# A graph layer on one core: the last but one node group's feed-forward moved behind the last edge pair, and another edge pair gathered ahead

## The chip, the cores and the metric

One core of a Trainium2 chip runs the program. Its engines work side by side, each through its own queue in order: PE (TensorE, matrix products and transposes), DVE (VectorE), ACT (ScalarE), POOL (GpSimd, here the issuer of gathers, DMAs whose rows are picked by a list of indices) and SP (SyncE, the issuer of all other DMAs). The metric is the device time of one execution in microseconds; several executions are timed and their median is taken. Separately one execution is profiled.

## What is computed

A graph attention layer over N = 12500 nodes and E = 400000 edges, sorted by destination, 128 features in 8 heads of 16, 32 features per edge. Cut to what matters:

```
h   = relu(layernorm(x))
x_l = ln1(h) @ W_l            x_r = ln1(h) @ W_r
per edge:  m     = leaky_relu(x_l[src] + x_r[dst] + edge_attr @ W_e)
           alpha = sum over a head of (m * att)
per node:  out   = sum(exp(alpha - max) * x_l[src]) / sum(exp(alpha - max))
           (each node has also an edge to itself, with the mean edge_attr)
h   = h + out + bias
y   = x + h + gelu(ln2(h) @ W1 + b1) @ W2 + b2
```

## The kernel before

Nodes are kept in 98 tiles of 128, edges are worked on in **pairs**: pair c holds edges 512 c to 512 c + 511, in four columns of 128. There are 782 pairs, 0 to 781, and the last has one column only.

**Prologue.** `tile_gnn` normalises x, multiplies it by W_l and writes the rows x_l to DRAM (`xl_dram`). While that runs, 29 pairs are served another way, since their rows of x_l do not exist yet: POOL gathers rows of x itself (`raw_gather`, L288) and they are stored in `raw_dram`. `raw_pairs` (L131) says which pairs: 24 at steps of 32 pairs (40, 72, ..., 744, 776) and `RAW_MORE` = 5 more, each 8 after one of the first of these (48, 80, 112, 144, 176).

**The edge loop.** `window_edges` writes its order out by hand. Time is counted in rounds r; the table `stages` says which step works in round r on which pair, so that on every engine the steps of several pairs alternate:

- r = c - 4, `gather` (L926): POOL issues four gathers from `xl_dram`, one per column, into the row buffer `xs` (12 buffers). For one of the 29 pairs SP loads the finished rows from `late_dram` instead (L921).
- r = c, `combine` (L980, L984): PE transposes the gathered rows and adds the products of the edge features and of the window of x_r.
- r = c + 1, `slope` (ACT, L998) and `bend` (DVE, L1003), the leaky relu; r = c + 2, `apart` (L991) and `score` (L1008) on PE; r = c + 3, `lowest` (DVE, L1014; L1017 for the short last pair) and `weigh` (ACT, the exponential, L1025); r = c + 4, `turn` (PE transposes, L1033); r = c + 5, `keep_turned` (ACT, L1038); r = c + 6, `collect` (PE, the weighted sums, L1047); r = c + 7, `own_heads` (DVE, L1056 and L1062) and `put` (SP, L1073), which writes each unit's sums into one of two `state` arrays in DRAM; writes into one array follow each other.

The last pair is combined in round 781, collected in 787, and put in 788.

**Rows gathered ahead.** For each of the 29 pairs, `raw_steps` (L609 to L691) runs twelve steps in twelve rounds, starting 17 rounds before the pair's own: load from `raw_dram` (SP), statistics, root, scale, relu, four transposes on PE (L651), copy and squares, variance, root, four products on PE (L672), rows, store to `late_dram` (SP).

**Node groups.** When all edges of a group of nodes have been put, the group's state is read back and the rest of the layer is done for it. `node_groups` makes 25 groups: three tiles, then 23 of four, then the end group of three. Ordinary groups follow the table `steps`, one step a round: `f_load` (x_l, x_r and x, on SP), `f_order` (ACT copy), `f_z` (PE, L1152 and L1156), `f_bend`, `f_state` (SP, L1123), `f_score`, `f_low` (L1187 to L1193), `f_exp`, `f_den`, `f_out` (DVE, L1214 to L1224), `f_h`, `f_stats`, `f_root`, `f_scale` (ACT, `hn`, L1260), `f_turn` (PE, L1271), `f_turned` (ACT, L1286), two `f_up` (PE, L1297), two `f_gelu` (ACT, L1312), `f_down` (PE, L1322), `f_store` (DVE, L1335 to L1339), `f_put` (SP, L1342). Their offsets run from -4 to 17, with `f_out` at 5 and `f_scale` at 9; the group of round 740 is the last of them.

The last but one group has round 772 and follows a denser table, `soon`: `f_load` at 768, `f_state` at 772, `f_low` and `f_exp` at 773, `f_den` and `f_out` at 774, `f_h` and `f_stats` at 775, `f_root` and `f_scale` at 776, `f_turn` at 777, the ups and gelus at 778 and 779, `f_down` at 780, `f_store` and `f_put` at 781. The end group has round 790 and follows `last_steps`: `f_load` at 772 up to `f_kept` at 777 (f_biases, L1136 and L1138, at 775), then `f_state` at 790 and all the rest at 791.

**PSUM rings and buffers.** `z`, `ab`, `pt_ps` and `acc` are rings of two banks each. Node steps borrow from them: `bank_of` takes one of `acc` if nothing else is said, and `f_out` one of `ab`. Most tiles of a node group have one buffer and are shared by all groups; the end group has its own `xo`, `x` and `sc`.

Of the kernel before, what the change touches and what calls it, by code (L numbers as in the profile page):

```python
# [53 lines left out]
AHEAD = 4  # L54
WAHEAD = 3
XR_STEPS = 6
RAW_MORE = 5
RAW_SHIFT = 8
RAW_STEPS = 12
TURN_AT = 13  # L60
# [48 lines left out]
def node_groups(nt):  # L109

    last = GN - 1
    first = (nt - last) % GN
    at = ([0] if first else []) + list(range(first, nt, GN))
    return [(t, n - t) for t, n in zip(at, at[1:] + [nt])]


def edges_per_node(nt, n_edges):
    return -(-n_edges // (nt * P))
# [7 lines left out]
def xr_round(t0, nt, n_edges):  # L126

    first = (t0 * P - CW) * edges_per_node(nt, n_edges) // U - SPARE
    return first // UP - WAHEAD - XR_STEPS - 1


def raw_pairs(nt, n_edges):

    n_pr = -(-n_edges // (UP * U))
    at = [xr_round(t, nt, n_edges) + XR_STEPS + 1 for t in range(GN, nt, GN)]
    at = at + [r + RAW_SHIFT for r in at[:RAW_MORE]]
    return [(r + RAW_STEPS + AHEAD + 1, r) for r in at if r + RAW_STEPS + AHEAD + 2 < n_pr]


# [9 lines left out]
def tile_gnn(  # L149
# [45 lines left out]
    dc_dram = dram.tile([RP * RU // UP * PW], BF16, name="dc_dram")  # L195
    du_dram = dram.tile([RP * RU * U], BF16, name="du_dram")
    raw = [{"c": c, "i": i, "round": r, "n": UP * KU} for i, (c, r) in enumerate(raw_pairs(NT, n_edges))]
    raw_dram = dram.tile([len(raw), P, UP * KU, P], F32, name="raw_dram")
    late_dram = dram.tile([len(raw), P, UP * KU, XW], F32, name="late_dram")
# [72 lines left out]
    def load_raw():  # L272
        step = GN * P * edges_per_node(NT, n_edges) // (UP * U)
        for part in (raw[: len(raw) - RAW_MORE], raw[len(raw) - RAW_MORE :]):
            assert all(d["c"] == part[0]["c"] + i * step for i, d in enumerate(part))
# [576 lines left out]
def window_edges(  # L852
# [30 lines left out]
    with ExitStack() as es:  # L883
# [218 lines left out]
        groups = [{"t0": t, "n": n, "ts": slice(t, t + n)} for t, n in node_groups(NT)]  # L1102
        end = groups[-1]

        def own_tile(d, name, shape, dt, tag=None, bufs=1):

            if d is end and name in ("xo", "x", "sc"):
                return fin.tile(shape(d["n"]), dt, name=f"end_{name}")
            return fin.tile(shape(GN), dt, name=f"f_{name}", tag=tag or f"f_{name}", bufs=bufs)

        def tiles(name, d, tag=None):
            d[name] = own_tile(d, name, lambda n: [P, n, P], F32, tag)
            return d[name][:, 0 : d["n"]]

        def bank_of(d, name, ring="acc"):
            d[name] = ps2.tile([P, EPR], F32, name=ring)
            return d[name]

        def f_state(d):
            n, ts = d["n"], d["ts"]  # L1120
            d["st"] = own_tile(d, "st", lambda n: [P, 2, n, SW], F32, "big", 3)
            for i in range(2):
                nc.sync.dma_start(d["st"][:, i, 0:n], state[i].rearrange("(t p h) f -> p t (h f)", p=P, h=H)[:, ts, :])  # L1123
# [104 lines left out]
        def f_h(d):  # L1228
            hb = h_sb[:, d["ts"], :].rearrange("p t f -> p (t f)")
            nc.vector.tensor_add(d["sum"], d["sum"], d["o2"])  # L1230
            if d is not end:
                up = d["sum"].rearrange("p (t f) -> p t f", f=P)
                nc.vector.tensor_add(up, up, bias_r[:, None, :].to_broadcast([P, d["n"], P]))
            nc.vector.tensor_add(hb, hb, d["sum"])
# [31 lines left out]
                )  # L1266

        def f_turn(d):
            tp = bank_of(d, "tp")
            for i in range(d["n"]):  # L1270
                nc.tensor.transpose(tp[:, i * P : (i + 1) * P], d["hn"][:, i, :], ident)  # L1271

# [20 lines left out]

        def f_up(k):
            def up(d):
                n, u = d["n"], bank_of(d, f"u{k}")
                nc.tensor.matmul(  # L1297
                    u[:, 0 : n * P],
                    w1_sb[:, k * P : (k + 1) * P],
                    d["hT"][:, 0:n].rearrange("p t f -> p (t f)"),  # L1300
                    start=True,
                    stop=True,
                )

            return up

        def f_gelu(k):
            def gelu(d):
                n = d["n"]
                if k == 0:  # L1310
                    d["gel"] = own_tile(d, "gel", lambda n: [P, 2, n * P], F32, "big", 3)
                nc.scalar.activation(  # L1312
                    d["gel"][:, k, 0 : n * P], d[f"u{k}"][:, 0 : n * P], AF.Gelu, bias=cols[:, 5 + k : 6 + k]
                )

            return gelu

        def f_down(d):
            y = bank_of(d, "y")
            for i in range(d["n"]):  # L1320
                for k in range(2):
                    nc.tensor.matmul(  # L1322
                        y[:, i * P : (i + 1) * P],
                        d["gel"][:, k, i * P : (i + 1) * P],
                        w2_sb[:, k, :],
                        start=(k == 0),
                        stop=(k == 1),
                    )

        def f_store(d):  # L1330
            n = d["n"]
            up = d["y"][:, 0 : n * P].rearrange("p (t f) -> p t f", f=P)
            d["out"] = y = tiles("yo", d, "f_b")
            if d is end:
                nc.vector.tensor_add(y, up, d["x"][:, 0:n])  # L1335
                return
            nc.vector.tensor_add(up, up, d["x"][:, 0:n])
            nc.vector.tensor_add(up, up, h_sb[:, d["ts"], :])
            nc.vector.tensor_add(y, up, b2_r[:, None, :].to_broadcast([P, n, P]))  # L1339

        def f_put(d):
# [41 lines left out]
            (8, f_root),  # L1383
            (9, f_scale),
            (10, f_turn),
            (11, f_turned),
            (12, f_up(0)),
            (13, f_up(1)),
            (13, f_gelu(0)),
            (15, f_down),  # L1390
            (16, f_store),
            (17, f_put),
        )
        up0, up1, gelu0, gelu1 = f_up(0), f_up(1), f_gelu(0), f_gelu(1)
        soon = (
            (-4, f_load),
            (-3, f_order),
            (-2, f_z),
            (-1, f_bend),
            (0, f_state),  # L1400
            (0, f_score),
            (1, f_low),
            (1, f_exp),
            (2, f_den),
            (2, f_out),
            (3, f_h),
            (3, f_stats),
            (4, f_root),
            (4, f_scale),
            (5, f_turn),  # L1410
            (5, f_turned),
            (6, up0),
            (6, gelu0),
            (7, up1),
            (7, gelu1),
            (8, f_down),
            (9, f_store),
            (9, f_put),
        )
        last_steps = (  # L1420
            (-18, f_load),
            (-17, f_order),
            (-16, f_z),
            (-15, f_bend),
            (-15, f_biases),
            (-14, f_score),
            (-13, f_kept),
            (0, f_state),
            (1, f_low),
            (1, f_exp),  # L1430
# [13 lines left out]
            (1, gelu1),  # L1444
            (1, f_down),
            (1, f_store),
            (1, f_put),
        )
# [8 lines left out]
        def in_round(r, table, groups=groups):  # L1457
            for k, f in table:
                for d in groups:
                    if d["round"] + k == r:  # L1460
                        f(d)
# [10 lines left out]
        with tc.manual_schedule():  # L1472
            for r in range(-AHEAD, max(last_round, groups[-1]["round"] + 18)):
                in_round(r, early, groups[:-2])
                for late, f in stages:
                    c = r - late
                    if 0 <= c < n_pr:
                        f(c)
                for late, f in sum_stages:
                    i, off = divmod(r - late, SUM_STEP)  # L1480
                    if off == 0 and 0 <= i < NL:
                        f(i)
                if r > 0 and r % CLEAR == 0 and r // CLEAR < NT // GT:
                    clear(r // CLEAR)
                in_round(r, steps, groups[:-2])
                in_round(r, soon, groups[-2:-1])
                in_round(r, last_steps, groups[-1:])
                in_round(r, enumerate(xr_steps), qs[1:])
                in_round(r, enumerate(raw_steps), raw)
                for late, f in late_stages:  # L1490
                    c = r - late
                    if 0 <= c < n_pr:
                        f(c)
# [354 lines left out]
```

## Time and profile before

| | |
|---|---|
| timed, median of 3 runs | 3979.37 us (3976.93 to 3980.35) |
| the profiled execution, its time | 3979.82 us |
| the profiled execution, its span | 3978.0 us |
| PE busy | 3535.5 us (89%) |
| DVE busy | 2996.7 us (75%) |
| POOL busy | 2961.1 us (74%) |
| ACT busy | 2177.6 us (55%) |
| granted TensorE clock, mean | 0.955 |

The span runs from the first instruction to the last, and the execution's time is 1.8 us longer. Busy shares are means over prologue, edge loop and end. Rows of the timeline give the start in us from the span's beginning, the busy time of a merged run of instructions, engine, line, operation, tiles and count, and in brackets the idle time ahead of it with what ended it. Rows of groups give the total busy time, the mean in ns of one, and the idle time ahead of them with its releasers. Rows of stages give from : to, the length, then each engine's busy time with its number of instructions (for a single line: of that line's engine alone), then the granted clock, the DMA share and GB/s.

### The profile page before, as it was taken

Reading aid. Unit: us, or ns where it says so; the run is one execution under the profiler, and the core shown is the slowest. Engines: PE = TensorE matmul, PEld = TensorE weight load, DVE = VectorE, ACT = ScalarE, POOL = GpSimd, SP = SyncE. Lnnn points to the kernel's source line nnn. Section 1 sums busy time; section 2 is a strip of 40 time slices with the busy share of each in tenths; the row PEclk is TensorE's granted clock in tenths of the full one; section 3 lists DMA queues with packets and bytes.
Section 4 is the critical chain, followed back from the end, with each engine's and each line's share of the span. In section 5 each row is a group of like instructions: output and inputs, shape, how many; then the busy total and the mean of one; then the engine's idle time right before and its main releaser. Section 6 shows DMA issues by size and latency. Waiting matters only on the chain.

```text
span 3978.0 us, 63158 instructions
## 1 busy us (share of the span) xinstructions
PE 3535.5 (89%) x18434; PEld 2235.4 (56%) x18435; DVE 2996.7 (75%) x6282; ACT 2177.6 (55%) x4746; POOL 2961.1 (74%) x3147
## 2 busy tenths in 40 slices
PE   2588899999999999999999999989999999999987
PEld 2355555555555556555665556656565655555554
DVE  6578888888878777777777777777777767767766
ACT  7445545555555545555555555556455555555554
POOL 7777777777777777777777777777777777777772
PEclk9799999999999999999999999999999999999998
DMA  7677777766655555555555555555555555555552
GB/s 207 210 176 175 182 190 179 165 161 154 151 103 114 109 112 112 109 110 108 104 110 115 109 110 111 113 109 108 112 104 107 110 115 97 110 110 100 107 104 63
DMA packets 625309, 502.69 MB, mean 126 GB/s; under 512 B 320174, under 2 KB 522013, under 8 KB 624717
## 3 DMA queue, kind: packets, MB, share of 16 engines
q1 hardware_dynamic: 524381, 281.11, 29.6%
q0 software_dynamic: 100000, 217.32, 27.7%
q8 instruction: 152, 2.49, 0.3%
q14 instruction: 200, 1.64, 0.1%
q10 hardware_dynamic: 576, 0.13, 0.0%
HBM read 432.27 MB, written 65.83 MB: 125 GB/s over the span
## 4 chain that ended last, share of the span: by engine, by line
PE 41%; POOL 20%; DMA 17%; issue 13%; DVE 7%; ACT 1%; SPq 1%; POOLq 0%; DVEq 0%; ACTq 0%
POOL xs L926 17%; DMA xs<-xl_dram,src_sb 14%; PE acc L1047 10%; PE z L984 10%; PE ab L1008 8%; PE pt_ps L1033 7%; PE z L980 4%; POOL raw L288 2%; DVE rec L1014 1%; DMA state<-rec 1%; DVE ea L967 1%; DVE m L1003 1%; PE acc L1322 1%; PE acc L1297 1%; DVE own L1056 1%
## 5 line engine op out<-in xcount | busy, mean ns | idle before, releaser
L926 POOL DMA_INDIRECT xs<-xl_dram,src_sb x3009 | 2842.4, 945 | 917.3 <-issue 790.1
L1025 ACT ACTIVATE p<-ab,rec 128x256 f32<-128x256 f32 x1563 | 654.8, 470 | 1026.9 <-DVE rec L1014 1011.6
L1047 PE MATMUL acc<-xs,pt 128*128 128x136 f32 x6250 | 904.6, 291 | 0.6 <-DVE f_m L1166 0.5
L984 PE MATMUL z<-ea,zw 64*128 64x512 f32 x1564 | 900.4, 656 | 3.8 <-DMA zw<-xr_dram 3.5
L980 PE MATMUL z<-ident,xs 128*128 128x128 f32 x3125 | 575.9, 285 | 291.0 <-DMA xs<-xl_dram,src_sb 260.3
L1056 DVE TENSOR_TENSOR own<-acc,diag 128x272 f32<-128x272 f32 x782 | 342.9, 438 | 652.5 <-PE acc L1047 646.5
L1008 PE MATMUL ab<-m,negrep 128*128 128x512 f32 x1564 | 833.5, 616 | 0.0
L1047 PEld LDWEIGHTS acc<-xs,pt 128*128 128x128 f32 x6250 | 828.8, 201 | 1.1 <-DVE f_m L1166 0.8
L980 PEld LDWEIGHTS z<-ident,xs 128*128 128x128 f32 x3125 | 406.9, 144 | 718.2 <-DMA xs<-xl_dram,src_sb 370.8
L1038 ACT COPY pt<-pt_ps 128x512 f32<-128x512 f32 x782 | 454.8, 582 | 573.1 <-PE pt_ps L1033 562.1
L1033 PEld LDWEIGHTS pt_ps<-ident,p 128*128 128x128 f32 x3125 | 340.5, 145 | 617.9 <-issue 510.1
L1003 DVE TENSOR_TENSOR m<-z,zs 128x512 f32<-128x512 f32 x782 | 532.8, 681 | 103.6 <-ACT zs L998 99.1
L967 DVE TENSOR_SCALAR ea<-dl,nid 32x516 f32<-32x516 bf16 x782 | 582.1, 744 | 29.0 <-DMA dl<-dc_dram 3.7
L1014 DVE TENSOR_REDUCE rec<-ab 128x2 f32<-128x512 f32 x781 | 538.8, 690 | 34.8 <-PE ab L1008 33.4
L1033 PE MATMUL pt_ps<-ident,p 128*128 128x128 f32 x3125 | 534.4, 296 | 2.6 <-ACT pt L1038 1.9
L998 ACT ACTIVATE zs<-z 128x512 f32<-128x512 f32 x782 | 472.0, 604 | 45.4 <-PE z L984 45.4
L1062 DVE TENSOR_REDUCE rec<-own 128x34 f32<-128x272 f32 x782 | 340.8, 436 | 26.7
L991 PE MATMUL ab<-ne,farw 64*128 64x512 bf16 x782 | 307.3, 393 | 31.2 <-ACT p L1025 27.4
L984 PEld LDWEIGHTS z<-ea,zw 64*128 64x128 f32 x1564 | 234.7, 188 | 122.3 <-issue 59.8
L1008 PEld LDWEIGHTS ab<-m,negrep 128*128 128x128 f32 x1564 | 252.8, 200 | 2.3 <-issue 2.3
L973 DVE TENSOR_SCALAR ne<-dl,nid 96x512 bf16<-96x512 bf16 x391 | 145.7, 373 | 12.7 <-DMA dl<-du_dram 0.3
L288 POOL DMA_INDIRECT raw<-in_x,src_raw x116 | 115.3, 994 | 38.8 <-issue 34.4
(206 smaller groups left out, 2163.2 us busy)
## 6 DMA issues: line engine op xcount, KB each, us to landing
ea<-in_ea_t SPq DMA_DIRECT2D x392, 128.0 KB
ea_s<-in_ea_t SPq DMA_DIRECT2D x98, 512.0 KB
xs<-xl_dram,src_sb POOLq DMA_INDIRECT x3009
dl<-dc_dram SPq DMA_DIRECT2D x392, 66.0 KB
state<-rec SPq DMA_DIRECT2D x1563, 9.0 KB
state<-empty SPq DMA_DIRECT2D x28, 504.0 KB
f_st<-state SPq DMA_DIRECT2D x46, 288.0 KB
dl<-du_dram SPq DMA_DIRECT2D x392, 32.0 KB
```

Source lines behind the costliest of these rows:

```text
L926: nc.gpsimd.indirect_dma_start(out=xs[:, j, :], out_offset=None, in_=xl_dram, in_offset=bass.IndirectOffsetOnAxis(ap=src_sb[:, c * KP + j ...
L967: nc.vector.tensor_scalar(d["ea"][rs].rearrange("p (a b) -> p a b", b=OW), d["dl"][rs].rearrange("p (a b) -> p a b", b=OS)[:, :, 0:OW], ni ...
L980: nc.tensor.matmul(z[:, j * P : (j + 1) * P], d["xs"][:, j, 0:P], ident, start=(j == 0), stop=False, is_transpose=True)
L984: nc.tensor.matmul(z[:, :e], d["zw"][rs], d["ea"][rs, :e], start=False, stop=True)
L998: nc.scalar.activation(d["zs"][:, :e], d["z"][:, :e], AF.Copy, scale=SLOPE)
L1003: nc.vector.tensor_tensor(d["m"][:, :e], d["z"][:, :e], d["zs"][:, :e], op=OP.max)
L1008: nc.tensor.matmul(d["ab"][:, :e], negrep.rearrange("p n h -> p (n h)"), d["m"][:, :e], start=False, stop=True)
L1014: nc.vector.tensor_reduce(d["rec"][:, :, CX], d["ab"].rearrange("p (u e) -> p u e", e=U), AX.X, OP.min)
L1025: nc.scalar.activation(d["p"][:, us], d["ab"][:, us], AF.Exp, bias=d["rec"][:, i, CX:SH], scale=-1.0)
L1033: nc.tensor.transpose(d["pt_ps"][:, js], d["p"][:, js], ident)
L1038: nc.scalar.copy(d["pt"][:, :e], d["pt_ps"][:, :e])
L1047: nc.tensor.matmul(d["acc"][:, i, :], d["pt"][:, j * P : (j + 1) * P], d["xs"][:, j, :], start=(j == js[0]), stop=(j == js[-1]),)
```

## The change

1. The list of pairs gathered ahead: pair 776 is dropped and 208 is added (`RAW_MORE` 6, and the last of the steps of 32 cut off). There are still 29.
2. The last but one group's table `soon` is stretched: `f_load` to `f_kept` in rounds 758 to 763, `f_state` at 772, then `f_low`, `f_exp`, `f_den`, `f_out`, `f_h`, `f_stats`, `f_root` one per round from 773 to 779, `f_scale` at 780.
3. Its feed-forward has a table of its own, `after`, counted from the end group's round 790: `f_ready` (an activation on one column that loads the gelu's table), `f_turn` and `f_turned` in 788, ups and gelus in 789, `f_down` and `f_store` in 790, `f_put` in 791. In each round they come ahead of the end group's steps of that round and behind the stages of the pairs.
4. As in the end group, the biases go into h and x early (`f_biases`), x + h is formed in `f_rest`, and `f_store` is then a single add.
5. Its banks come from other rings: `f_turn` and the ups from `z`, `f_down` from `ab`.
6. The end group's early steps move to rounds 764 to 769.

```diff
-RAW_MORE = 5
+RAW_MORE = 6
...
-    at = at + [r + RAW_SHIFT for r in at[:RAW_MORE]]
+    at = at[:-1] + [r + RAW_SHIFT for r in at[:RAW_MORE]]
...
+        def near_end(d):
+            return any(d is g for g in groups[-2:])
...
         def f_h(d):
-            if d is not end:
+            if not near_end(d):
...
-            tp = bank_of(d, "tp")
+            tp = bank_of(d, "tp", "z" if d is groups[-2] else "acc")
...
-                n, u = d["n"], bank_of(d, f"u{k}")
+                n, u = d["n"], bank_of(d, f"u{k}", "z" if d is groups[-2] else "acc")
...
-            y = bank_of(d, "y")
+            y = bank_of(d, "y", "ab" if d is groups[-2] else "acc")
...
         def f_store(d):
-            if d is end:
+            if near_end(d):
                 nc.vector.tensor_add(y, up, d["x"][:, 0:n])
                 return
...
         soon = (
-            (-4, f_load), (-3, f_order), (-2, f_z), (-1, f_bend),
-            (0, f_state), (0, f_score), (1, f_low), (1, f_exp),
-            (2, f_den), (2, f_out), (3, f_h), (3, f_stats),
-            (4, f_root), (4, f_scale), (5, f_turn), (5, f_turned),
-            (6, up0), (6, gelu0), (7, up1), (7, gelu1),
-            (8, f_down), (9, f_store), (9, f_put),
+            (-14, f_load), (-13, f_order), (-12, f_z), (-11, f_bend),
+            (-11, f_biases), (-10, f_score), (-9, f_kept),
+            (0, f_state), (1, f_low), (2, f_exp), (3, f_den),
+            (4, f_out), (5, f_h), (6, f_stats), (7, f_root),
+            (8, f_scale), (8, f_rest),
+        )
+        after = (
+            (-2, f_ready), (-2, f_turn), (-2, f_turned),
+            (-1, up0), (-1, up1), (-1, gelu0), (-1, gelu1),
+            (0, f_down), (0, f_store), (1, f_put),
         )
         last_steps = (
-            (-18, f_load), (-17, f_order), (-16, f_z), (-15, f_bend),
-            (-15, f_biases), (-14, f_score), (-13, f_kept),
+            (-26, f_load), (-25, f_order), (-24, f_z), (-23, f_bend),
+            (-23, f_biases), (-22, f_score), (-21, f_kept),
...
                 in_round(r, soon, groups[-2:-1])
+                for k, f in after:
+                    if end["round"] + k == r:
+                        f(groups[-2])
                 in_round(r, last_steps, groups[-1:])
```

(The tables of the diff are set several entries to a line here.)

More of the change, by code (lines that the diff above doesn't have):

```diff
@@ L1395, in window_edges @@
         soon = (
[L1396 to L1399, printed above, removed]
+            (-14, f_load),
+            (-13, f_order),
+            (-12, f_z),
+            (-11, f_bend),
+            (-11, f_biases),
+            (-10, f_score),
+            (-9, f_kept),
             (0, f_state),
-            (0, f_score),
             (1, f_low),
[L1403 to L1418, printed above, removed]
+            (2, f_exp),
+            (3, f_den),
+            (4, f_out),
+            (5, f_h),
+            (6, f_stats),
+            (7, f_root),
+            (8, f_scale),
+            (8, f_rest),
+        )
+        after = (
+            (-2, f_ready),
+            (-2, f_turn),
+            (-2, f_turned),
+            (-1, up0),
+            (-1, up1),
+            (-1, gelu0),
+            (-1, gelu1),
+            (0, f_down),
+            (0, f_store),
+            (1, f_put),
         )
         last_steps = (
[L1421 to L1427, printed above, removed]
+            (-26, f_load),
+            (-25, f_order),
+            (-24, f_z),
+            (-23, f_bend),
+            (-23, f_biases),
+            (-22, f_score),
+            (-21, f_kept),
             (0, f_state),
```

## The prediction

> **What bounds the kernel now.** I read the costliest groups first, for POOL.
>
> ```profile
> span 3978.0 us, 63158 instructions
> ...
> L926 POOL DMA_INDIRECT xs<-xl_dram,src_sb x3009 | 2842.4, 945 | 917.3 <-issue 790.1
> ```
>
> POOL issues 3009 gathers of rows. The idle time ahead of them is 917.3 / 3009 = 0.305 us each, almost all "issue". So a gather costs 0.945 + 0.305 = 1.25 us and a pair, four of them, 5.0 us. Next, the stages, for these gathers alone, then the POOL timeline.
>
> ```profile
> 200.00:700.00 500.00, 378.04 (x401) 0.95 0.74 180
> ...
> 2200.00:3200.00 1000.00, 756.11 (x801) 0.97 0.54 110
> ...
> 3700.00:3900.00 200.00, 151.21 (x161) 0.97 0.55 113
> ```
> ```profile
> 158.44 0.94 POOL L926 DMA_INDIRECT xs<-xl_dram,src_sb  x1 [0.30 <-issue]
> ...
> 2605.93 0.94 POOL L926 DMA_INDIRECT xs<-xl_dram,src_sb  x1 [0.31 <-issue]
> ...
> 3755.35 0.94 POOL L926 DMA_INDIRECT xs<-xl_dram,src_sb  x1 [0.30 <-issue]
> ...
> 3765.33 0.94 POOL L926 DMA_INDIRECT xs<-xl_dram,src_sb  x1 [0.30 <-issue]
> ...
> 3850.24 0.94 POOL L926 DMA_INDIRECT xs<-xl_dram,src_sb  x1 [0.30 <-issue]
> ...
> 3915.62 0.94 POOL L926 DMA_INDIRECT xs<-xl_dram,src_sb  x1 [0.30 <-issue]
> 3916.87 0.94 POOL L926 DMA_INDIRECT xs<-xl_dram,src_sb  x1 [0.30 <-issue]
> ```
>
> The rate never changes (401 in 500 us, 161 in 200 us) and (3916.87 - 158.44) / 3008 is again 1.25 us: **POOL never stops between its first gather and its last.** The rows above are, in order, the first gather, the last gathers of pairs 509, 747, 749, 766 and 780, and the single gather of 781 (counted back from the end: four a pair, one for 781, none for a pair gathered first). Beside them, TensorE's transposes (L980) of the same pairs:
>
> ```profile
> 2609.54 0.33 PE L980 MATMUL z<-ident,xs 128*128 128x128 f32 x1 [0.89 <-DMA xs<-xl_dram,src_sb]
> ...
> 3762.38 0.81 PE L980 MATMUL z<-ident,xs 128*128 128x128 f32 x4
> ...
> 3766.45 0.60 PE L980 MATMUL z<-ident,xs 128*128 128x128 f32 x4
> ...
> 3770.31 0.60 PE L980 MATMUL z<-ident,xs 128*128 128x128 f32 x4
> ...
> 3852.77 0.33 PE L980 MATMUL z<-ident,xs 128*128 128x128 f32 x1 [0.24 <-DMA xs<-xl_dram,src_sb]
> ...
> 3931.74 0.60 PE L980 MATMUL z<-ident,xs 128*128 128x128 f32 x4
> ...
> 3937.39 0.27 PE L980 MATMUL z<-ident,xs 128*128 128x128 f32 x1
> ```
>
> I call **lag** the time from the start of a pair's last gather to the end of its transposes. It is 3.9 us at pair 509, 7.8 at 747, 5.6 at 749, 2.9 at 766 (TensorE waits for the rows there), but 3932.34 - 3915.62 = 16.7 at 780 and 3937.66 - 3916.87 = 20.8 at 781. Up to 766 the kernel goes at POOL's pace; over the last fifteen rounds TensorE falls 18 us behind a stream that has no more to give. The stall rows of those rounds say why:
>
> ```profile
> 3900.18 0.68 DVE L1214 TENSOR_TENSOR f_o<-f_xo,acc 128x512 f32<-128x512 f32 x1
> 3900.78 0.43 DVE L1056 TENSOR_TENSOR own<-acc,diag 128x272 f32<-128x272 f32 x1
> ```
> ```profile
> 3900.96 0.52 PE L1152 MATMUL acc<-ident,f_xl 128*128 128x128 f32 x3 [2.52 <-issue]
> ...
> 3918.52 0.63 PE L1271 MATMUL acc<-ident,f_hn 128*128 128x128 f32 x4 [2.33 <-DVE end_sc L1178]
> ...
> 3922.17 2.02 PE L1047 MATMUL acc<-xs,pt 128*128 128x136 f32 x8
> ...
> 3930.88 1.02 PE L1297 MATMUL acc<-f_hT,w_sb 128*128 128x512 f32 x2
> ...
> 3935.60 1.95 PE L1322 MATMUL acc<-w_sb,f_gel 128*128 128x128 f32 x16
> ```
>
> Both last node groups are worked on together there: f_z of the end group waits 2.52 us and goes on when VectorE, busy with the other's f_out until then, has begun the next own_heads; f_turn waits 2.33 us for its normalised rows, TensorE then runs at half clock (2.02 us for L1047 x8, 1.09 in other rounds), and the products themselves take their time. Pair 776, whose rows come without POOL, adds a TensorE round with no POOL time beside it.
>
> After the last sum the path is short and serial:
>
> ```profile
> 3946.65 2.25 PE L1047 MATMUL acc<-xs,pt 128*128 128x136 f32 x18
> ...
> 3953.52 0.93 SPq L1123 DMA_DIRECT2D f_st<-state  x2
> ...
> 3956.88 0.20 DVE L1187 TENSOR_TENSOR f_mn<-f_st 128x24 f32<-128x24 f32 x1 [6.72 <-DMA f_st<-state]
> ...
> 3957.85 0.26 ACT L1196 ACTIVATE f_wt<-f_wt 128x72 f32<-128x72 f32 x1 [10.74 <-DVE f_wt L1193]
> ...
> 3965.49 1.24 PE L1271 MATMUL acc<-ident,f_hn 128*128 128x128 f32 x3 [16.59 <-ACT f_hn L1260]
> ```
>
> Call T = 3948.90 the end of the last sum. f_low of the end group starts at T + 8.0, its f_exp at T + 8.95, its first TensorE work at T + 16.6, and the span ends at T + 29.1.
>
> **The change part by part.**
>
> *Pair 776 given up, 208 taken.* Still 29 pairs gathered first, so still 116 early gathers and 3009 late ones. POOL's last gather stays at 3916.87; between pairs 208 and 776 it is one pair, 5.0 us, earlier than now, and TensorE, which waits for rows, comes with it. The steps of L609 to L691 move, with their store to DRAM and the load on SP's queue, from rounds 759 to 770 to rounds 191 to 202. There 208 costs a TensorE round of 3.86 us (3766.45 to 3770.31) that POOL does not wait for, besides its own products; a raised lag falls by 5.0 - 3.86 = 1.1 us a round. POOL would be held only where TensorE is some 23 us late: twelve row buffers let it run six pairs ahead of the sums. Cost there: nothing.
>
> *Node work earlier, spread out.* f_load to f_kept of the last but one group go to rounds 758 to 763, the end group's to 764 to 769, so the two no longer meet; f_low to f_scale are one per round in 773 to 780, as in the ordinary groups. VectorE does as many adds as before (the bias of f_h and two of f_store's three go to f_biases and f_rest). The f_load transfers on SP, and any gather they slow, lie ten rounds earlier and are recovered. One side effect:
>
> ```profile
> 3909.09 1.23 POOL L926 DMA_INDIRECT xs<-xl_dram,src_sb  x1 [0.30 <-DMA xs<-xl_dram,src_sb]
> ...
> 3908.96 0.55 DVE L1138 TENSOR_TENSOR end_x<-end_x,b_r 128x384 f32<-128x384 f32 x1
> ```
>
> Beside this add of two SBUF operands a gather took 1.23 us, 0.29 more than usual; the add of the same kind just before cost none. The change puts two more of them (f_biases) beside the stream: between 0 and 0.6 us on its end, I take **+0.3**. The Trainium skill (GPSIMD Engine Reference, 1. Specifications) says that GpSimd shares its SBUF interfaces with VectorE and contends with instructions of two SBUF inputs; this row agrees.
>
> *Lag at the last pair.* With the groups apart and no pair without gathers near, rounds 771 to 781 look like those of earlier groups. f_out stands at 776, f_scale at 780; in the group of round 740 the place of 780 is pair 749 (lag 5.6, still carrying raw pair 744), in that of round 500 it is pair 509 (3.9, none near). I take 4.5. Before, pair 781 followed 780 by 3937.66 - 3932.34 = 5.32 us, of which 1.79 (3935.60 to 3937.39) were f_down's products, now gone: 3.53, less the 1.25 between the two gathers. So the lag at 781 is 4.5 + 3.53 - 1.25 = 6.8 instead of 20.8: **14.0 us earlier**. Best, with the 2.9 of pair 766 at 780: 15.6. Worst, with the 7.8 of pair 747: 10.7.
>
> *Rounds 782 to 787* are TensorE work without a gap now (3937.39 to T, 11.5 us) and stay so; a stretch of half clock as at 3922.17 may fall there or not.
>
> ```profile
> 3920.00:3940.00 20.00, 20.00 (x96) 12.91 (x94) 11.86 (x21) 14.33 (x24) 0.00 (x0) 0.83 0.03 4
> ```
>
> The granted clock of that window, 0.83, is 20 x 0.17 / 0.5 = 6.8 us at half rate, which does the work of 3.4 us; I take 0 and keep 3.4 for the range.
>
> *Products behind T.* New on the path's neighbours, priced by rows:
>
> ```profile
> 3919.18 0.78 ACT L1286 ACTIVATE f_hT<-acc,cols 128x512 f32<-128x512 f32 x1 [0.61 <-PE acc L1271]
> ...
> 3931.05 1.28 ACT L1312 ACT_TABLE_LOAD   x1
> 3932.35 0.69 ACT L1312 ACTIVATE f_gel<-acc,cols 128x512 f32<-128x512 f32 x1
> ...
> 3937.77 0.69 DVE L1337 TENSOR_TENSOR acc<-acc,f_x 128x512 f32<-128x512 f32 x1
> ...
> 3946.32 0.79 ACT L1038 COPY pt<-pt_ps 128x512 f32<-128x512 f32 x2
> ```
>
> f_turn 0.63, f_turned 0.78, f_up 2 x 1.02, the second gelu 0.69, f_down 1.95, f_store's one add 0.69: 6.8, with handoffs 7.1 us after T. The wait it adds is on VectorE, where f_store now stands in front of the end group's f_low; that needs T + 8.0, so 0.9 us are left and the cost is **0**. ScalarE is free from 3947.11, so f_ready's table load (1.28) lies beside the last sums; Exp's load ends near T + 6.5, ahead of T + 8.95. On SP, f_put goes behind both f_st loads. If TensorE were at half clock, its 4.6 us of this double and 3.7 us come out on the path. No gain comes here either: nothing in the end group's chain got shorter.
>
> **Sum.** -14.0 + 0.3 = -13.7. The profiled execution took 3979.82 us (span 3978.0), 0.45 over the median of the three timed runs, 3979.37; from that median 3965.7.
>
> **The rivals.**
>
> A. *Only the products go.* The lag comes from ScalarE and VectorE, and spreading does not cure it; TensorE saves 0.63 + 2 x 1.02 + 1.95 = 4.6. Time 3974.8. For it: f_turn waited for ScalarE and VectorE. Against it: ordinary groups do the same work at lags of 4 to 8.
>
> B. *The stream gets longer.* If POOL stands still near pair 208, the 5.0 us of 776's gathers are added at the end: 3970.7. Against it: no pause anywhere in 3009 gathers with 28 such pairs about.
>
> C. *The end chain pays.* The products run at half clock and f_store holds f_low: +3.7, 3969.4. It decides from T + 8.0. For it: between f_turn, f_up and f_down TensorE has two gaps of 0.7 to 0.8 us (f_turned, the second gelu).
>
> D. *The half clock stays (slower).* Paced by POOL, TensorE idles 1.1 us in each round; if the clock fell for that and stayed, a round would cost 7.7 instead of 5.0 over 776 to 780 (13.6), the drained rounds 11.5 more, the products 3.7: 28.8 - 13.7 = 15.1, 3994.5. From the rows, an idle of 2.33 us came ahead of the half clock, waits of 0.24 and 0.89 us are those of paced rounds, and the clock over the paced stages is 0.95 to 0.97; so it would need some 2 us of idle in every round. The Trainium skill (TensorE: Matmul & The Clock Gate, HAM oscillation) describes such a loop, half rate again after every gap of over some 3.4 us; the trace falls earlier than that figure, but 1.1 us is below both.
>
> That 208's stretch costs POOL nothing is in B; that the change does less than it says is not open, since the instruction order shows every move.
>
> **How the numbers follow.** Forecast 0.68, A 0.12, B 0.06, C 0.10, D 0.04. A measurement of this kernel tells about 0.2%, 8 us, from no change, so faster means below 3971.4: forecast, B and C, 0.84; A is within, 0.12; D is slower, 0.04. The range reaches from the best lag with the scatter of the runs (3979.4 - 15.6 - 1.8 = 3962) to the worst lag with a half-clock stretch and a little of C (3979.4 - 10.7 + 3.4 = 3972, rounded to 3973); it leaves out A and D, 0.16.
>
> **What would show it.** POOL: 3009 gathers, no pause, last one at 3916.6 to 3917.5. TensorE: pair 781 transposed some 7 us after its gather instead of 20.8, about 3924; no L1271 or L1297 of the last but one group before the last sum; T near 3935. VectorE: f_yo of that group done before f_st has landed, f_low at T + 8. A last gather later than 3919 is B, a lag over 12 is A, f_low later than T + 8.5 is C, L1047 x8 at 2.0 us round after round is D.

## The result, and the profile after

The changed kernel takes 3966.9 us (median of 8 runs, 3965.01 to 3968.32), the kernel before, timed beside it on the same chip, 3978.72 (8 runs, 3976.54 to 3980.35): a ratio of 0.997, interval 0.9962 to 0.9979, **11.8 us faster**. The profiled execution took 3966.68 us with a span of 3964.9, 13.1 below the span of before; the granted clock is 0.955 in both.

First the page's head and its costliest group, and the end of the POOL timeline (the last gathers of pairs 780 and 781):

```profile
span 3964.9 us, 63156 instructions
...
L926 POOL DMA_INDIRECT xs<-xl_dram,src_sb x3009 | 2842.8, 945 | 917.2 <-issue 767.1
```
```profile
3916.04 0.94 POOL L926 DMA_INDIRECT xs<-xl_dram,src_sb  x1 [0.30 <-issue]
3917.29 0.94 POOL L926 DMA_INDIRECT xs<-xl_dram,src_sb  x1 [0.30 <-issue]
```

Still 3009 gathers at the same price, the last one 0.4 us later than before (3917.29 against 3916.87). Then TensorE from there to the end; from L1123 of the kernel before on, lines are three further down here (f_low L1190, f_turn L1274, ups L1300, f_down L1325):

```profile
3918.55 0.33 PE L980 MATMUL z<-ident,xs 128*128 128x128 f32 x1 [0.88 <-DMA xs<-xl_dram,src_sb]
...
3922.14 0.27 PE L980 MATMUL z<-ident,xs 128*128 128x128 f32 x1
...
3931.40 2.25 PE L1047 MATMUL acc<-xs,pt 128*128 128x136 f32 x18
3933.49 0.60 PE L1274 MATMUL z<-ident,f_hn 128*128 128x128 f32 x4
3934.96 1.98 PE L1300 MATMUL z<-f_hT,w_sb 128*128 128x512 f32 x4 [0.87 <-ACT f_hT L1289]
...
3937.72 1.83 PE L1325 MATMUL ab<-w_sb,f_gel 128*128 128x128 f32 x14 [0.37 <-ACT f_gel L1315]
...
3953.54 2.93 PE L1300 MATMUL acc<-f_hT,w_sb 128*128 128x384 f32 x4 [0.77 <-DVE f_hT L1282]
...
3957.14 2.40 PE L1325 MATMUL acc<-w_sb,f_gel 128*128 128x128 f32 x10 [0.24 <-ACT f_gel L1315]
```

TensorE waits for the rows of pair 780 again (0.88 us, releaser the gather's DMA), so it keeps up with POOL: the lag is 3918.88 - 3916.04 = 2.84 us at 780 and 3922.41 - 3917.29 = 5.12 at 781, where it was 16.7 and 20.8. T, the end of the last sum, is 3933.65, 15.25 earlier than before. The feed-forward of the last but one group stands behind it at full clock. VectorE and ScalarE after T:

```profile
3939.58 0.69 DVE L1338 TENSOR_TENSOR f_yo<-ab,f_x 128x512 f32<-128x512 f32 x1 [4.68 <-PE ab L1325]
3941.74 0.20 DVE L1190 TENSOR_TENSOR f_mn<-f_st 128x24 f32<-128x24 f32 x1 [1.46 <-DMA f_st<-state]
```
```profile
3949.05 1.28 ACT L1254 ACT_TABLE_LOAD   x1 [6.23 <-DVE f_rstd L1251]
3950.34 0.20 ACT L1254 ACTIVATE f_rstd<-f_rstd 128x3 f32<-128x3 f32 x1
```

f_store's add is done 1.46 us before the end group's state lands; f_low starts at T + 8.09 (T + 7.98 before), 15.1 us earlier than there. But of these 15.1 only 13.1 reach the end of the span. Two places of the end group's chain got longer; here are their counterparts in the kernel before:

```profile
3958.13 1.28 ACT L1251 ACT_TABLE_LOAD   x1
3964.29 0.20 ACT L1251 ACTIVATE f_rstd<-f_rstd 128x3 f32<-128x3 f32 x1 [4.88 <-DVE f_rstd L1248]
```
```profile
3971.10 1.38 PE L1322 MATMUL acc<-w_sb,f_gel 128*128 128x128 f32 x10 [0.24 <-ACT f_gel L1312]
```

- **The root's table load.** Before, it ran right behind the exponential and was done 4.88 us before the root; after, it waits for VectorE's f_rstd (L1251) and its 1.28 us stand in the chain. The root starts at T + 16.69 instead of T + 15.39: 1.3 lost.
- **Half clock in the last products.** Ten of the end group's f_down products take 2.40 us instead of 1.38. From the root to the end of these products it is 9.20 us (3950.34 to 3959.54) instead of 8.19: 1.0 lost.

### The profile page after: what moved, and what is told of

It is laid out like the page before. It is cut to its first block, busy times and chain, and to the rows that moved or that the text cites. A ratio compares the mean times of both kernels' runs of the same rounds, so it can differ in the third digit from the quotient of the medians.

```text
span 3964.9 us, 63156 instructions
## 1 busy us (share of the span) xinstructions
PE 3542.0 (89%) x18434; PEld 2239.1 (56%) x18435; DVE 2997.8 (76%) x6283; ACT 2174.3 (55%) x4745; POOL 2961.2 (75%) x3147
## 5 line engine op out<-in xcount | busy, mean ns | idle before, releaser
L1047 PE MATMUL acc<-xs,pt 128*128 128x136 f32 x6250 | 905.6, 290 | 0.0
L984 PE MATMUL z<-ea,zw 64*128 64x512 f32 x1564 | 897.1, 654 | 2.8 <-DMA zw<-xr_dram 2.8
L1008 PE MATMUL ab<-m,negrep 128*128 128x512 f32 x1564 | 833.5, 615 | 0.0
L980 PE MATMUL z<-ident,xs 128*128 128x128 f32 x3125 | 582.0, 285 | 281.4 <-DMA xs<-xl_dram,src_sb 243.2
L1047 PEld LDWEIGHTS acc<-xs,pt 128*128 128x128 f32 x6250 | 829.8, 201 | 0.0
L980 PEld LDWEIGHTS z<-ident,xs 128*128 128x128 f32 x3125 | 407.3, 143 | 715.8 <-DMA xs<-xl_dram,src_sb 371.3
L1033 PEld LDWEIGHTS pt_ps<-ident,p 128*128 128x128 f32 x3125 | 339.7, 144 | 614.1 <-issue 505.7
L1033 PE MATMUL pt_ps<-ident,p 128*128 128x128 f32 x3125 | 533.6, 295 | 1.9 <-ACT pt L1038 1.3
L991 PE MATMUL ab<-ne,farw 64*128 64x512 bf16 x782 | 306.5, 392 | 34.6 <-ACT p L1025 30.8
L984 PEld LDWEIGHTS z<-ea,zw 64*128 64x128 f32 x1564 | 233.8, 187 | 121.2 <-issue 57.5
L1008 PEld LDWEIGHTS ab<-m,negrep 128*128 128x128 f32 x1564 | 253.5, 200 | 3.0 <-issue 3.0
```

Source lines behind the costliest of these rows:

```text
L980: nc.tensor.matmul(z[:, j * P : (j + 1) * P], d["xs"][:, j, 0:P], ident, start=(j == 0), stop=False, is_transpose=True)
L984: nc.tensor.matmul(z[:, :e], d["zw"][rs], d["ea"][rs, :e], start=False, stop=True)
L1008: nc.tensor.matmul(d["ab"][:, :e], negrep.rearrange("p n h -> p (n h)"), d["m"][:, :e], start=False, stop=True)
L1033: nc.tensor.transpose(d["pt_ps"][:, js], d["p"][:, js], ident)
L1047: nc.tensor.matmul(d["acc"][:, i, :], d["pt"][:, j * P : (j + 1) * P], d["xs"][:, j, :], start=(j == js[0]), stop=(j == js[-1]),)
```

## The experiments

Theory: POOL paces the kernel up to its last gather, and the end then follows at the lag that TensorE has built up by the last pair; the change takes the lag away and leaves POOL's stream as it is. Rivals: only the products' place matters, whatever the lag comes from; or the stream itself got shorter or longer. A second question came with the trace: what the two losses at the end are made of.

A condition has to be told first. On three chips the kernel *before* took 4829.29, 4775.05 and 4820.31 us, 20 to 21% more. Here are two groups on TensorE and one on POOL of the kernel before with the list change alone, on one of these chips, and then the two TensorE groups of the changed kernel on the chip of the result (total busy time, mean, idle time ahead with its releasers):

```profile
L1047 PE MATMUL acc<-xs,pt 128*128 128x136 f32 x6250 | 1018.6, 309 | 176.5 <-issue 120.2 <-DVE own L1056 45.1 <-DVE f_yo L1339 3.3
...
L980 PE MATMUL z<-ident,xs 128*128 128x128 f32 x3125 | 521.0, 291 | 289.1 <-issue 91.6 <-remote 70.0 <-PE ab L1008 67.9
```
```profile
L926 POOL DMA_INDIRECT xs<-xl_dram,src_sb x3009 | 2840.1, 944 | 1697.7 <-issue 789.6
```
```profile
L1047 PE MATMUL acc<-xs,pt 128*128 128x136 f32 x6250 | 905.6, 290 | 0.0
...
L980 PE MATMUL z<-ident,xs 128*128 128x128 f32 x3125 | 582.0, 285 | 281.4 <-DMA xs<-xl_dram,src_sb 243.2 <-DMA zw<-xr_dram 9.9 <-DMA state<-rec 9.7
```

On the chip of the result the sums (L1047) never wait and the transposes (L980) wait for gathered rows. On the other one, TensorE waits for "issue" ahead of both, hardly for rows, and POOL idles 1697.7 instead of 917.3 us. Of this idle time 608 us end with a TensorE instruction of the edge loop (L1047 alone 219.3, then L1033, L1008, L980 and L984): there **TensorE paces and POOL waits** for it. The price of a gather is the same (944 ns). What sits behind "issue" the profile doesn't say, so what slows TensorE there stays open. Runs on these chips test the theory in a kernel whose bound is another; they don't measure the change in question.

**e1_swap and e1b_swap: the list alone.** The kernel before, with this edit:

```diff
-RAW_MORE = 5
+RAW_MORE = 6
-    at = at + [r + RAW_SHIFT for r in at[:RAW_MORE]]
+    at = at[:-1] + [r + RAW_SHIFT for r in at[:RAW_MORE]]
```

> The kernel before with the list of early pairs alone changed (208 for 776). Theory D (distance): what counts is how far TensorE stands behind POOL's stream at pair 781. Rounds up to 775 come 5.0 us earlier, and the raw steps of 776 no longer sit in rounds 759 to 770, but rounds 776 to 781 keep their collisions (35.1 us from the transposes of 775 to those of 781): pair 781's transposes end at about 3931 instead of 3937.7, time 6 to 7 us below before, about 3972. Theory W (work): each part removes its own work from the end and the parts add up; the swap is worth the 5.0 us of one pair's gathers, 3973.7, and the rest belongs to the tables. Theory S: the swap does nearly all, 3967.

> The swap alone once more, since on the first chip TensorE, not POOL, paced even the kernel before (4829 us). Where before takes about 3978: theory D (distance behind POOL's stream) 6 to 7 us below before, pair 781's transposes end near 3931; theory W (parts add up) 5.0 below; theory S (the swap does nearly all) 12 below.

Both came to chips where TensorE paces: 4826.26 against 4829.29, ratio 0.9998 (0.9989 to 1.0007), and 4771.08 against 4775.05, 0.9992 (0.9982 to 1.0001). No difference where POOL doesn't pace, as it must be if the list moves POOL's time and leaves TensorE's work as it was; for the question itself both are inconclusive.

**e2_tables, e2b_tables and e2c_tables: all but the list.** The changed kernel with the old list (the edit above, reversed).

> The changed kernel with the list of early pairs as before (776 early, 208 not). Theory D: with the groups apart TensorE follows POOL up to 775, pair 776 adds one round of 3.9 us and f_out beside it a stall as in the group of round 740, so the lag at 780 is that of pair 749 (5.5) and at 781 about 7.8: 2 to 3 us behind the changed kernel, 10 us below before, about 3969. Theory W: without the swap's 5.0 us, 3971.9. Theory S: close to before, 3978.

> The tables alone once more (776 early, 208 not). Where before takes about 3978: theory D 10 us below before, lag at 781 about 7.8; theory W 7 below; theory S close to before.

> The tables alone, 776 still gathered early and 208 not, a third time, since on the chips so far TensorE paced the kernel before (4829 and 4775 us). Where before takes about 3978: theory D (distance behind POOL's stream) 10 us below before, lag at 781 about 7.8 against 5.1 in the changed kernel; theory W (parts add up) 7 below; theory S (the swap does nearly all) close to before.

The first two came to TensorE-paced chips: ratios 0.9984 (0.9975 to 0.9992) and 0.9985 (0.9975 to 0.9994). The third came to a chip where POOL paces: 3972.67 (11 runs) against 3979.65 (15 runs), 0.9982 (0.9973 to 0.9991), 7.0 us faster. In its trace TensorE waits 2.41 us in the round after 776, and runs at half clock behind it:

```profile
3913.17 0.37 PE L991 MATMUL ab<-ne,farw 64*128 64x512 bf16 x1 [2.41 <-ACT p L1025]
...
3915.43 1.91 PE L1008 MATMUL ab<-m,negrep 128*128 128x512 f32 x2
...
3920.44 1.02 PE L1008 MATMUL ab<-m,negrep 128*128 128x512 f32 x2
...
3929.03 0.27 PE L980 MATMUL z<-ident,xs 128*128 128x128 f32 x1
```
```profile
3920.36 0.94 POOL L926 DMA_INDIRECT xs<-xl_dram,src_sb  x1 [0.30 <-issue]
```

L1008 x2 takes 1.91 us, and 1.02 a round later. The lag at 781 is 3929.30 - 3920.36 = 8.9 us: between the 20.8 of before and the 5.1 of the whole change. So the tables take 11.9 us of lag away and the list 3.8 more. The 8.9 isn't scatter: in the four profiles with the new list and the spread node work (after, e5, e6, e8) it is 5.1 to 5.2. The lags of single pairs show the way from one to the other. In e2c it is 2.9 us at pair 775, 5.6 at 777 (776 is a TensorE round with no gather beside it), 8.9 at 778 behind the wait of 2.41, then 1.1 less per round, 6.6 at 780. In the changed kernel it stays between 2.8 and 3.1 from 775 to 780. The span is 6.4 us below that of before: 11.9 of lag, less 3.5 for a later last gather and 2.0 for a longer way from T to the end (the table below). Of the expectation's theories S, with no change, is out; the time is W's 7, and its interval (3.6 to 10.7 us) holds D's 10 too, whose lag of 7.8 is near the measured one.

**e3_late and e3b_late: the products alone.** The changed kernel with the old list, the dense `soon` and the old `last_steps`, so that the feed-forward stands elsewhere and little else changes (the early biases, the single add of f_store and the other banks stay):

```diff
-RAW_MORE = 6
+RAW_MORE = 5
-    at = at[:-1] + [r + RAW_SHIFT for r in at[:RAW_MORE]]
+    at = at + [r + RAW_SHIFT for r in at[:RAW_MORE]]
         soon = (
-            (-14, f_load), ... (-9, f_kept), (0, f_state), (1, f_low),
-            (2, f_exp), ... (8, f_scale), (8, f_rest),
+            (-4, f_load), ... (-1, f_biases), (0, f_state), (0, f_score),
+            (1, f_low), (1, f_exp), ... (4, f_scale), (4, f_rest),
         last_steps = (
-            (-26, f_load), ... (-21, f_kept),
+            (-18, f_load), ... (-13, f_kept),
```

> The kernel before with the last but one group's products alone moved behind the last sum (its f_load to f_scale stay dense in rounds 768 to 776, the end group's early steps stay at 772 to 777, 776 stays early). Theory D: TensorE no longer waits 2.33 us in f_turn, the half clock that followed goes too, and 4.6 us of products: rounds 777 to 781 take about 16 instead of 25.4 us, 9 us; of it 1.3 (the root's table load, which the changed kernel shows on the path) and about 1 (half clock in the last f_down) are lost at the end: 7 us below before, 3972. Theory W: the 4.6 us of the products less those 2.3, about 3976.

> The products alone moved behind the last sum, once more (first it ran on a chip where TensorE paced the kernel before, 4829 us). Where before takes about 3978: theory D (distance behind POOL's stream) 7 us below before, since with the products the wait of f_turn and the half clock behind it go too; theory W (parts add up) 2.3 us below, the 4.6 of the products less what the end loses.

Both on TensorE-paced chips: 4822.45 against 4829.29, 0.9986 (0.9977 to 0.9995), and 4814.85 against 4820.31, 0.9985 (0.9976 to 0.9993). By the ratios that is as much as e2 and e2b, which spread the node work as well; the intervals are too wide to tell 5.5 and 6.8 us in the medians here from 9.2 and 6.7 there.

**e4_spread: the list and the spreading, the products in rounds 781 to 786.**

```diff
+            (9, f_turn), (9, f_turned), (10, up0), (10, gelu0), (11, up1),
+            (11, gelu1), (12, f_down), (13, f_store), (14, f_put),
         )
-        after = ( ... )
+        after = ()
```

> The changed kernel with the products of the last but one group in rounds 781 to 786 instead of behind the last sum. Theory D: the lag at 781 stays that of the changed kernel, but the products (4.6 us of TensorE) and the gelu's two table changes between the exponentials stand in the rounds that drain, while the root's table load at the end is hidden again (-1.3): 3 to 7 us above the changed kernel, 3970 to 3974. Theory W: 4.6 less 1.3, 3970. If the place behind the last sum is worth nothing: 3965.6.

On the same chip as e1 to e3: 4830.12 against 4829.29, 1.0004 (0.9994 to 1.0014). Where TensorE paces, then, the list and the spreading gained nothing with the products in these rounds, and the products behind the last sum gained 5.5 to 6.8 us in the medians of e3. That the spreading alone is worth nothing there isn't shown: in e4 the gelu's table loads also stand between the exponentials of the last pairs, and what they cost wasn't measured.

**e7_gathers: POOL's pace.** In 40 pairs one gather of the four is left out (the products take another column's rows):

```diff
-                for j in t:
+                for j in t[:1] if c % 4 == 2 and 300 <= c < 460 and t[0] else t:
...
```

> The changed kernel, with one gather of four left out in each of 40 pairs between 302 and 458 (the fourth column uses the third's rows, so these edges' sums are not the layer's). If POOL's stream paces the kernel, 40 x 1.25 = 50 us less: 3917, and the last gather near 3867. If TensorE paced it, no change, since it does the same work.

```profile
L926 POOL DMA_INDIRECT xs<-xl_dram,src_sb x2969 | 2804.4, 945 | 905.3 <-issue 765.9
...
```
```profile
3867.59 0.94 POOL L926 DMA_INDIRECT xs<-xl_dram,src_sb  x1 [0.30 <-issue]
```

3916.11 us (two runs): 50.2 below e5, which ran beside it, for 40 gathers of 1.25 us, all of them over 1500 us ahead of the end. The last gather comes 49.7 us earlier than in the changed kernel. So POOL paces, and TensorE follows it all the way.

**e5_ready: the root's wait.** In the changed kernel the last but one group's f_ready (L1278) reads `rstd`, which all groups share, on ScalarE. My reading is that the end group's root, which overwrites it, then waits for ScalarE's own earlier reading besides VectorE, and that one of the two waits, the one for VectorE, comes to stand in front of the table load. The edit lets f_ready read a constant column instead:

```diff
-            nc.scalar.activation(..., d["rstd"][:, 0:1], AF.Gelu)
+            of = d["rstd"] if d is end else cols[:, 2:3]
+            nc.scalar.activation(..., of[:, 0:1], AF.Gelu)
```

> The changed kernel, with f_ready of the last but one group reading a constant column instead of that group's rstd. In the changed kernel the end group's root has two waits (VectorE and ScalarE's own), and the first stands ahead of its table load, so 1.28 us of load lie on the path. With one wait the load runs right behind f_exp: 1.3 us less than the changed kernel, 3965.6, and the load starts near 3943 instead of 3949. If the load waits for another reason: no change.

```profile
3943.99 1.28 ACT L1254 ACT_TABLE_LOAD   x1
3950.16 0.20 ACT L1254 ACTIVATE f_rstd<-f_rstd 128x3 f32<-128x3 f32 x1 [4.89 <-DVE f_rstd L1251]
```

The load is back behind the exponential; the root starts at T + 15.2 and from T to the end it is 29.8 us instead of 31.25. So it is shown that the reading of `rstd` exposes the load; that it does so by a second wait is argued, since the profile doesn't list the waits themselves. The time, 3966.34 against 3977.69 of before on that chip, 0.9972 (0.9962 to 0.9982), doesn't tell it from the changed kernel's 0.997: in the profile POOL's last gather came 1.35 us later (below).

**e6_warm: the half clock.** e5 and eleven products into an unused bank, read by nobody, behind the last but one group's f_down:

```diff
+        def f_idle(d):
+            bank = ps2.tile([P, EPR], F32, name="pt_ps")
+            for i in range(11):
+                nc.tensor.matmul(bank, w1_sb[:, 0:P], h_sb[:, 0:GN, :]..., start=True, stop=True)
...
             (0, f_store),
+            (0, f_idle),
```

> As the one with f_ready changed, and 11 products of 128x512 into an unused bank behind f_down of the last but one group, results unread, which keep TensorE busy until the end group's f_turn. If the half clock there (2.93 us for the ups, 2.40 for the last ten of f_down) is due to TensorE's idle time: full clock, 2.2 to 2.6 us less than that kernel, 3963.2. If the clock does not follow, or the added products still run when f_turn comes: same or up to 3 us more.

```profile
3940.25 9.61 PE L1338 MATMUL pt_ps<-h_sb,w_sb 128*128 128x512 f32 x22
3951.05 1.10 PE L1274 MATMUL acc<-ident,f_hn 128*128 128x128 f32 x3 [1.19 <-ACT f_hn L1263]
3952.91 1.56 PE L1301 MATMUL acc<-f_hT,w_sb 128*128 128x384 f32 x4 [0.77 <-DVE f_hT L1283]
...
3955.14 1.38 PE L1326 MATMUL acc<-w_sb,f_gel 128*128 128x128 f32 x10 [0.16 <-ACT f_gel L1316]
```

The end group's ups take 1.56 instead of 2.93 us and the ten f_down products 1.38 instead of 2.40. From T to the end it is 27.45 us, 2.3 less than e5 and 1.65 less than before. Time 3963.72 (7 runs, 3962.73 to 3966.36) against 3977.69: ratio 0.9969 (0.9958 to 0.998), which doesn't tell it from the changed kernel's 0.997. It is 2.6 us under e5 on the same chip, with intervals that overlap; what carries the reading is the chain in the trace.

**e8_slack: how much the products may grow.** The changed kernel and six unread products between the ups and f_down (`(-1, f_idle)` behind `up1`, with six in place of eleven).

> The changed kernel, with 6 products of 128x512 into an unused bank between the ups and f_down of the last but one group, results unread: TensorE's f_down ends about 3.6 us later. f_yo was done 1.46 us before f_low's data (3940.28 and 3941.74). If f_store in front of f_low on VectorE is the wait that decides: f_low about 2.1 us later, time 3969. If the products behind the last sum hide whatever their length: no change.

```profile
3937.48 5.31 PE L1337 MATMUL pt_ps<-h_sb,w_sb 128*128 128x512 f32 x12
```
```profile
3944.62 0.69 DVE L1344 TENSOR_TENSOR f_yo<-ab,f_x 128x512 f32<-128x512 f32 x1 [9.00 <-PE ab L1325]
3945.22 0.20 DVE L1190 TENSOR_TENSOR f_mn<-f_st 128x24 f32<-128x24 f32 x1
```

f_store's add starts at T + 10.26 instead of T + 5.93, 4.3 later; f_low follows it without a wait at T + 10.86, 2.8 later. The difference, 1.5, is the slack that the row of f_low shows in the changed kernel (1.46). The expectation had f_low 2.1 us later, since it put the six products at 3.6. From T to the end 34.0 us, 2.7 more; time 3970.25, against 3966.9 for the changed kernel on the chip of the result. So f_store does stand ahead of f_low, and rival C's point of decision is where it was put; the change stays short of it.

The profiles on chips where POOL paces, side by side (T as above; the first gather's start varies with the execution):

| | first gather | last gather | lag at 781 | T | T to end | span |
|---|---|---|---|---|---|---|
| before | 158.44 | 3916.87 | 20.8 | 3948.90 | 29.1 | 3978.0 |
| after | 158.56 | 3917.29 | 5.1 | 3933.65 | 31.25 | 3964.9 |
| e2c | 159.59 | 3920.36 | 8.9 | 3940.54 | 31.1 | 3971.6 |
| e5 | 159.08 | 3918.64 | 5.1 | 3934.98 | 29.8 | 3964.8 |
| e6 | 158.45 | 3918.12 | 5.2 | 3934.52 | 27.45 | 3962.0 |
| e8 | 158.71 | 3917.98 | 5.1 | 3934.36 | 34.0 | 3968.3 |

Last gather less first, it is 3758.4 us before and 3758.7 to 3760.8 in the others. Most of this is f_biases: its two adds of two SBUF operands, here in e2c, and the gather beside them:

```profile
3837.47 0.68 DVE L1139 TENSOR_TENSOR h_sb<-h_sb,bias_r 128x512 f32<-128x512 f32 x1
3838.07 0.68 DVE L1141 TENSOR_TENSOR f_x<-f_x,b_r 128x512 f32<-128x512 f32 x1
```
```profile
3837.39 2.18 POOL L926 DMA_INDIRECT xs<-xl_dram,src_sb  x1 [0.30 <-issue]
```

The gather begins just ahead of the adds, which last 1.28 us together, and takes 2.18 instead of 0.94, 1.24 more. In the changed kernel's own profile it is 1.46, since the gather begins when the second add does:

```profile
3825.31 1.46 POOL L926 DMA_INDIRECT xs<-xl_dram,src_sb  x1 [0.30 <-issue]
...
3855.78 1.13 POOL L926 DMA_INDIRECT xs<-xl_dram,src_sb  x1 [0.30 <-issue]
```

In the six profiles of the table eleven gathers start while these adds run, or 0.08 us ahead of them as here, and each gains the time from its start to the end of the adds, less 0.12 to 0.13 us. Of the six that start 0.46 to 0.91 us ahead of an add and still run when it begins, five gain nothing and one 0.06. So a gather that starts beside the adds stands still until they end, and one that is half done goes on; the execution's phase decides which it is.

## Why the prediction was right, and where its terms were off

It gave 3965.7 with a range of 3962 to 3973; the median is 3966.9. Step by step:

- **POOL bounds the kernel and goes on without a pause.** Right: 3009 gathers, the last one at 3917.29, inside the 3916.6 to 3917.5 given; e7 shows the pace by itself. Rival B, a stream made longer near pair 208, did not come.
- **The lag at the last pair (-14.0).** The mechanism was right, the size somewhat small: -15.7. The mis-sized term is the lag at 780, put at 4.5 after the steps of earlier groups and measured at 2.84, which is the "best" case of pair 766. The step from 780 to 781 was 2.28 to the hundredth (3.53 - 1.25).
- **The adds of f_biases (+0.3, 0 to 0.6).** Right in kind and, in the profile after, in size: the gathers beside the adds gained 0.71 us there, against 0.29 before, 0.4 more. But the upper end of the range was too low: in e2c they gained 1.83, 1.5 more. The estimate took the price from one gather that started 0.42 us before the end of the add, where a gather can start up to 1.36 before the end of both (e2c). The section of the Trainium skill cited there agrees in kind; it gives no size.
- **Rounds 782 to 787.** Right: from 781's transposes to T it is 11.24 us in both (3922.41 to 3933.65, 3937.66 to 3948.90).
- **The products behind T (0).** Right: f_low at T + 8.09; the add ended 6.6 us after T, 0.5 ahead of the estimate, and e8 shows the slack. Rival C would have begun at T + 8.5.
- **"Nothing in the end group's chain got shorter".** True, but the step asked only that: it did not ask whether something got longer, and two things did. f_ready's reading of `rstd` exposed the root's table load: 1.3 us, undone by e5. And TensorE came back to full clock at T + 25.65 instead of T + 22.1 (the granted clock is 0.50 up to 3959.3 and 1.00 behind it, before 0.50 up to 3971.0), too late for most of the last f_down: 1.0, undone by e6 together with the half clock that the kernel before has there too. The prediction weighed the half clock for the last but one group's products, where it did not fall. That all groups share `rstd` stood in the kernel, and the load's 1.28 us in the quoted rows: the question could have been asked before.
- **Rival A, only the products go.** On the chip in question the lag fell to 5.1, not to over 12, so more than the products went. On the chips where TensorE paces, A is nearer to what happened: by the ratios e3 gained as much as e2, and e4 nothing (with the reserve told there).
- **Rival D, the half clock stays.** From 3760 us to T it fell once, for 3.4 us at 3880.8, and not round after round.

The sum in the profile: -15.7 (lag) + 0.4 (last gather) + 1.3 + 1.0 leaves -13.0; the spans differ by 13.1. In the medians it is 11.8, in an interval of 8.4 to 15.1. Two errors of opposite sign, 1.7 too little gain and 2.3 of loss not seen, let the forecast come as near as it did; that part is luck.

**What stays open.** The list, the products and the spreading were not each measured alone on a chip where POOL paces; there it is 7.0 us for products and spreading together and 11.8 for all, and the lags (8.9 and 5.1) give the list its share in a kernel that has the new tables. How the 7.0 divides isn't known. The changed kernel as a whole was not run on a chip where TensorE paces. Why the exponential came 2.4 us late in e2c's round of pair 777 wasn't followed up. Nor is it known why three chips run the kernel with TensorE as its pace.

## What to carry to other kernels

Find the stream that never pauses, and measure how far the engines behind it have fallen back when it ends: only that lag, and the serial chain after it, can be won near the end, and moving work out of the last rounds wins it even if the work is done later. When a step is put in front of a serial chain, list what it shares with it, buffers read on the same engine above all: here an activation's reading of a shared buffer pulled the next one's table load out from under cover (1.3 us). And an idle engine ahead of the last products costs clock; cheap work that nobody reads can keep it up (1.65 us better than the kernel before from the last sum on).

## What had not been expected of the hardware

- A gather on POOL took up to 2.18 us instead of 0.94 beside two VectorE adds of two SBUF operands that last 1.28 together: started beside them, it waits for their end, rather than being slowed by some share.
- The granted clock falls soon after TensorE stops. In the loop, waits of 2.33 us (before, L1271) and 2.41 (e2c, L991) stood just ahead of a stretch at half rate. At the end, the windows from 3940 to 3950 of the changed kernel and of e6 (length, PE busy, clock, DMA share, GB/s):

```profile
3940.00:3950.00 10.00, 0.00 (x0) 0.61 0.19 58
```
```profile
3940.00:3950.00 10.00, 9.86 (x26) 1.00 0.24 71
```

  0.61 is 7.8 us at half rate, so it fell at 3942.2, 2.65 us after the last product (3937.72 + 1.83). The Trainium skill (TensorE: Matmul & The Clock Gate, Part 1: The HAM clock gate) gives an idle window of about 3.4 us; here it was less. That busy time keeps the clock up, e6 shows.
- The same kernel on other chips of the kind was bound by another engine, 20% slower, with gathers at the same 0.944 us; a change that moves POOL's work (e1) then shows nothing, and one that moves TensorE's (e3) shows 5.5 to 6.8 us.
